# Layer 0 feed forward of a decoder: quarters of a batch against halves, with scaling on POOL and normalisation on ACT

## The chip, the cores and the metric

The kernel runs on one core of one Trainium2 chip. Its time is device microseconds (us) of one execution, and what is told is the median of several runs of the same build. Five engines work side by side and meet only through semaphores: TensorE (PE, its weight loads shown apart as PEld), VectorE (DVE), ScalarE (ACT), GpSimd (POOL) and SyncE (SP, which issues most DMAs). Each engine takes its own instructions strictly in order, so an instruction that waits holds up all that stand behind it on its engine.

## The reference

The input is x of 4 batches x 1024 tokens x 256 channels, with a context of 154 tokens per batch. Two decoder layers follow each other. Each has self attention, cross attention and a feed forward, and after each of the six parts x becomes layernorm(x + part). The change touches the feed forward of layer 0 and the normalisation behind its cross attention. What that feed forward computes:

```
def bit_linear(x, w):                      # act_quant: per token 127 / max|x|, rounded
    xq = x + (act_quant(x) - x)            # weight_quant: one scale, values -1, 0, 1
    wq = w + (weight_quant(w) - w)
    return einsum('bsd,hd->bsh', xq, wq)
h = bit_linear(x, w1)                      # 256 -> 1024
h = depthwise_conv1d(h)                    # three taps along the tokens, plus a bias
h = silu(h)
return bit_linear(h, w2)                   # 1024 -> 256
```

The second `act_quant` needs, for every token, the largest |h| over all 1024 hidden channels before anything can be rounded.

## The kernel before

The kernel has three stages in order of time. The first is layer 0's self attention (to about 690 us from the start of the span). The second is layer 0's cross attention, to about 1328 us, with a long tail. The third is layer 1: a self attention of full width to about 1730 us, then its cross attention and feed forward. The feed forward of layer 0 has no stage of its own. It is woven into the second half of layer 0's cross attention (batches 0 and 1) and into layer 1's self attention (batches 2 and 3).

The weaving is written by hand as events. `at(when, f, args)` puts a small piece of work at a place in a common order, and `run_in_order` calls all pieces in that order. One unit of `when` in the second stage is one call of `scores(s, j)`: four heads of 128 queries against 154 keys. There are 128 of these, 32 to a batch. `schedule(b, t0, length, start)` spreads the feed forward of batch b over `length` units from `t0`, in shares of 100. With `ends = (54, 92, 130, start + 1.2 T, start + 2.8 T)`, `start` 139 and `T` 25, batch 0 has units 54 to 92, batch 1 92 to 130, batch 2 130 to 169, batch 3 169 to 209. PE's instructions and some DMAs keep the order of the program (`tc.keep_in_program_order`). The order on the other engines is laid out by the framework's scheduler when the program is built.

One unit of cross attention: PE forms scores in one of two large PSUM tiles (`slot`); DVE takes their maximum (L810); ACT takes the exponential of four heads with their sums (L814); DVE takes the reciprocal (L818); POOL divides (L822, L825) into one of five `p` tiles; 3.4 units later PE transposes p (L839, L842) into two of four PSUM banks (`bank`), which DVE (L840) and ACT (L843) copy out. Every four units, `weighted` multiplies with the values and ACT copies two `ot` tiles (L860, 15 buffers); every sixteen units, four `out_projected` calls (L862) turn 512 tokens' `ot` into x, at 13.45, 17.45, 21.45 and 23.45 units after their last step, and are followed by `layernorm`.

The feed forward of a batch before the change, in four quarters r of N = 256 tokens:

- `token_scales` (L931, one reduce over the batch), `quantised_x` and `token_rows` (two halves), `edge_tokens`.
- `hidden(b, r, m)`, m from 0 to 3, takes two blocks of 128 hidden channels at once. PE makes 128 x (2 x 256) into one bank, DVE scales it by token into `ht` (L997), ACT fills the two edge columns (L1002) and does the middle tap per block (L1007, 256 columns), DVE the two outer taps per block (L1011, 256 columns each), and ACT a tanh (L1014). `gated` follows on DVE (L1021), with ACT's absolute value (L1026, L1028) and DVE's running maximum (L1029; the two block rows are joined in L1031).
- `hidden_scales` (PE transposes, DVE L1038 and four tiny operations), `quantised_hidden` (PE spreads the scales over all partitions in PSUM, then one DVE multiplication of 128x2048 against that PSUM bank, L1048, and one rounding to bfloat16 of 128x2048, L1051), `fed_forward` (PE, then DVE L1063), `layernorm(b, 2 * r, 2)`.

`layernorm` ends with one instruction per 128 tokens, six events later: on DVE (L169) or, with `scalar=True`, on ACT (L165) after a tiny DVE operation (L160). Before the change only layer 1 passes `scalar=True`. The large tile `gt` of the feed forward has one buffer, as have `xq`, `gq` and `xqT`.

Of the kernel before, what the change touches and what calls it, by code (L numbers as in the profile page):

```python
# [29 lines left out]
def decoder_kernel(ctx: ExitStack, tc: tile.TileContext, a: dict, out: bass.AP):  # L30
# [643 lines left out]
    def wide_cross_attention(wk, wf, slot, bank):  # L674
# [25 lines left out]
        def weight_loaded(name):  # L700
            w = wf.tile([P, 8, E], F32, tag="gt", name="wf", bufs=1).rearrange("p c n -> p (c n)")
            src = a[name].rearrange("(c p) n -> p c n", p=P)
            pe(nc.sync.dma_start(out=w.rearrange("p (c n) -> p c n", c=src.shape[1]), in_=src))
            asum = small.tile([P, 4], F32, tag="asum", name="asum")
            sc = small.tile([P, 1], F32, tag="wsc", name="wsc")
            floats[name] = w, asum, sc
# [138 lines left out]
        def weighted(s):  # L845
# [12 lines left out]
            for i in range(2):  # L858
                ots[s, i] = wk.tile([P, 512], F32, tag="ot", name="ot", bufs=15)
                nc.scalar.copy(ots[s, i], os[i])  # L860

        def out_projected(b, qh, k):  # L862
# [7 lines left out]
            if k == 3:  # L870
                layernorm(b, 4 * qh, 4)
# [19 lines left out]
        for s in range(8 * NB):  # L891
# [6 lines left out]
            if s % 4 == 3:  # L898
                for k in range(4):
                    last = s == 8 * NB - 1  # L900
                    at(4 * s + (10.7 + k if last else (13.45, 17.45, 21.45, 23.45)[k]), out_projected, s // 8, s // 4 % 2, k)


    def feed_forward(wf, bank):
# [7 lines left out]
        scs, dqs, xqTs, rows, edges, gts, ams, sc2s, dq2s, gqs, ths = ({} for _ in range(11))  # L912
        Q = 4
        N = S // Q

        def act_scales(amax, wmean):

            n = amax.shape[1]
            am = small.tile([P, n], F32, tag=f"am{n}", name="am", bufs=2)
            nc.vector.tensor_scalar(am, amax, 1e-5, None, ALU.max)  # L920
            sc = small.tile([P, n], F32, tag=f"sc{n}", name="sc", bufs=2)
            nc.vector.reciprocal(sc, am)
            nc.vector.tensor_scalar(sc, sc, 127.0, None, ALU.mult)
            dq = small.tile([P, n], F32, tag=f"dq{n}", name="dq", bufs=2)
# [3 lines left out]
        def token_scales(b):  # L928
            settle(b)
            amax = small.tile([P, NC], F32, tag="amax", name="amax", bufs=2)  # L930
            nc.vector.tensor_reduce(amax, xs[b], AX.X, ALU.max, apply_absolute_value=True)  # L931
            scs[b], dqs[b] = act_scales(amax, w1m)

        def quantised_x(b, q):
            if q == 0:
                xqTs[b] = wf.tile([P, 2, S], BF16, tag="xqT", name="xqT", bufs=1)
            t = bank(BF16)
            xr = wf.tile([P, 8, N], F32, tag="gt", name="xr", bufs=1)[:, :4, :]
            nc.vector.tensor_tensor(
                xr, xs[b][:, 4 * q : 4 * q + 4, :],  # L940
                scs[b][:, 4 * q : 4 * q + 4].unsqueeze(2).to_broadcast([P, 4, E]), ALU.mult,
            )

            xq = wf.tile([P, 4, E], BF16, tag="xq", name="xq", bufs=1)
            nc.vector.tensor_scalar(xq, xr, RND, RND, ALU.add, ALU.subtract)
            for e in range(2):
                for j in range(4):
                    o = t[:, e * 512 + j * P : e * 512 + (j + 1) * P]
                    pe(nc.tensor.transpose(o, xq[:, j, e * P : (e + 1) * P], ident_bf))
            nc.scalar.copy(xqTs[b][:, :, q * 512 : (q + 1) * 512], t.rearrange("p (e n) -> p e n", e=2))  # L950

        def token_rows(b, q):


            if q == 0:
                rows[b] = wf.tile([P, S], F32, tag="dqr", name="dqr", bufs=1)
            t = bank()
            for j in range(4):
                c = 4 * q + j
                pe(nc.tensor.transpose(  # L960
                    t[:, j * P : (j + 1) * P], dqs[b][:, c : c + 1].to_broadcast([P, P]), ident
                ))
            nc.scalar.copy(rows[b][:, q * 512 : (q + 1) * 512], t)

        def edge_tokens(b):

            t = bank()
            beside = lambda r: r[:, N - 1 : N - 1 + 3 * N].rearrange("p (q n) -> p q n", n=N)[:, :, 0:2]
            for hc in range(8):
                o = t[:, 8 * hc : 8 * hc + 6].rearrange("p (q n) -> p q n", n=2)  # L970
                for e in range(2):
                    mm(o, w1q[:, e, hc * P : (hc + 1) * P], beside(xqTs[b][:, e, :]), e == 0, e == 1)

            ed = edges[b] = wf.tile([P, 8, 2 * Q + 2], F32, tag="ed", name="ed", bufs=1)
            nc.gpsimd.memset(ed, 0.0)
            dq = small.tile([P, 3, 2], F32, tag="dqe", name="dqe", bufs=2)
            nc.vector.tensor_copy(dq, beside(rows[b]))
            nc.vector.tensor_tensor(
                ed[:, :, 2 : 2 * Q],
                t[:, :64].rearrange("p (c n) -> p c n", c=8)[:, :, :6],  # L980
                dq.rearrange("p q n -> p (q n)").unsqueeze(1).to_broadcast([P, 8, 6]), ALU.mult,
            )

        def hidden(b, r, m):
            if m == 0:
                gts[b, r] = wf.tile([P, 8, N], F32, tag="gt", name="gt", bufs=1)
            t = bank()
            for i in range(2):
                hc = 2 * m + i
                for e in range(2):  # L990
                    mm(
                        t[:, i * N : (i + 1) * N], w1q[:, e, hc * P : (hc + 1) * P],
                        xqTs[b][:, e, r * N : (r + 1) * N], e == 0, e == 1,
                    )

            ht = wf.tile([P, 2, N + 2], F32, tag="ht", name="ht", bufs=2)
            nc.vector.tensor_tensor(  # L997
                ht[:, :, 1 : N + 1], t.rearrange("p (i n) -> p i n", i=2),
                rows[b][:, r * N : (r + 1) * N].unsqueeze(1).to_broadcast([P, 2, N]), ALU.mult,
            )  # L1000
            for c, k in ((0, 2 * r), (N + 1, 2 * r + 3)):
                nc.scalar.copy(ht[:, :, c : c + 1], edges[b][:, 2 * m : 2 * m + 2, k : k + 1])  # L1002
            g2 = gts[b, r][:, 2 * m : 2 * m + 2, :]
            for i in range(2):
                hc = 2 * m + i
                g = g2[:, i, :]
                nc.scalar.activation(  # L1007
                    g, ht[:, i, 1 : N + 1], AF.Identity, bias=cb[:, hc : hc + 1], scale=cw[:, hc, 1:2]
                )
                for k in (0, 2):  # L1010
                    nc.vector.scalar_tensor_tensor(  # L1011
                        g, ht[:, i, k : k + N], cw[:, hc, k : k + 1], g, ALU.mult, ALU.add
                    )
            nc.scalar.activation(ht[:, :, :N], g2, AF.Tanh)  # L1014
            ths[b, r, m] = ht

        def gated(b, r, m):

            g2 = gts[b, r][:, 2 * m : 2 * m + 2, :]
            th = ths.pop((b, r, m))  # L1020
            nc.vector.scalar_tensor_tensor(g2, th[:, :, :N], 1.0, g2, ALU.add, ALU.mult)  # L1021
            if m == 0:
                ams[b, r] = wf.tile([P, 2, N], F32, tag="xq", name="am", bufs=1)
            am = ams[b, r]
            if m == 0:
                nc.scalar.activation(am, g2, AF.Abs)  # L1026
            else:
                nc.scalar.activation(th[:, :, :N], g2, AF.Abs)  # L1028
                nc.vector.tensor_tensor(am, am, th[:, :, :N], ALU.max)  # L1029
            if m == 3:  # L1030
                nc.vector.tensor_tensor(am[:, 0, :], am[:, 0, :], am[:, 1, :], ALU.max)  # L1031

        def hidden_scales(b, r):
            t = bank()
            for j in range(2):
                pe(nc.tensor.transpose(t[:, j * P : (j + 1) * P], ams[b, r][:, 0, j * P : (j + 1) * P], ident))
            amax = small.tile([P, 2], F32, tag="amax2", name="amax2", bufs=2)
# [687 lines left out]
```

## Time and profile before

| what | value |
|---|---|
| time, median of 3 runs (lowest to highest) | 2192.05 us (2190.69 to 2195.32) |
| the profiled execution's own time | 2189.57 us |
| its span | 2187.8 us |
| PE, DVE, ACT, POOL busy, share of the span | 94%, 66%, 51%, 27% |
| cross attention with the feed forward of batches 0 and 1 (948 to 1308 us) | PE 329.8, DVE 309.8, ACT 231.6, POOL 170.6 us busy of 360 |
| layer 1 self attention with the feed forward (1327 to 1640 us) | PE 287.8, DVE 243.0, ACT 151.9, POOL 16.7 us busy of 313 |

The busy time of an engine is the union of its instructions. A matmul is pipelined and counts as busy until its modelled end, so PE's share is not a share of its peak. "Idle before, releaser" says how long an engine stood still ahead of a group and what ended that.

### The profile page before, as it was taken

What the parts mean: (1) busy time and instruction counts of PE and PEld (TensorE: products, weight loads), DVE (VectorE), ACT (ScalarE), POOL (GpSimd) and SP (SyncE); (2) the same over time, 40 slices, a digit from 0 to 9 for tenths busy, and PEclk for the clock granted to TensorE, in tenths of its full rate; (3) what the DMA queues carried; (4) which work ended last, traced back from release to release, by engine and by line L of the source; (5) the groups of instructions that cost most, each with busy time, mean ns of one, the idle gap of its engine ahead of it and who ended that gap; (6) DMA issues with size and microseconds to landing.
All of it is one profiled execution on the core that took longest, in us unless ns stands there. A gap on an engine that the chain in (4) does not pass through costs nothing.

```text
span 2187.8 us, 38074 instructions
## 1 busy us (share of the span) xinstructions
PE 2056.9 (94%) x14062; PEld 1221.0 (56%) x14062; DVE 1450.1 (66%) x3179; ACT 1120.3 (51%) x2907; POOL 581.8 (27%) x1211
## 2 busy tenths in 40 slices
PE   7999999999998999989989889899989999999996
PEld 5545545545443556655655556666666655555554
DVE  6666676676673565578987987977762556564634
ACT  1555545545544565566656764545542234544444
POOL 1111231241234655454454442000000310111111
PEclk9999999999999999999999999999999999999998
DMA  4221211211201100000001000000000000010101
GB/s 123 65 56 55 70 36 36 51 36 26 61 27 20 40 21 1 1 1 1 1 1 35 1 23 1 1 1 1 1 1 0 12 15 16 10 30 11 30 1 39
DMA packets 34921, 52.29 MB, mean 24 GB/s; under 512 B 11697, under 2 KB 25905, under 8 KB 34737
## 3 DMA queue, kind: packets, MB, share of 16 engines
q1 hardware_dynamic: 32736, 48.18, 9.0%
q8 instruction: 112, 1.84, 0.3%
q10 hardware_dynamic: 2000, 1.68, 0.3%
q14 instruction: 73, 0.59, 0.1%
HBM read 19.23 MB, written 4.42 MB: 11 GB/s over the span
## 4 chain that ended last, share of the span: by engine, by line
PE 64%; DVE 22%; ACT 6%; POOL 4%; issue 2%; DMA 2%; SPq 1%; ACTq 0%; POOLq 0%; DVEq 0%
PE s L195 18%; PE t L653 14%; PE s L1261 11%; PE s L653 7%; PE acc L195 5%; DVE gt L1011 4%; PE acc L1261 3%; ACT u L814 2%; PE t L839 2%; DVE nmp L361 2%; DVE nmx L810 1%; DVE bnst L136 1%; DVE x L169 1%; DVE ht L997 1%; POOL y L521 1%
## 5 line engine op out<-in xcount | busy, mean ns | idle before, releaser
L422 ACT ACTIVATE p<-s 128x512 f32<-128x512 f32 x576 | 311.8, 596 | 274.6 <-PE s L195 274.1
L361 DVE TENSOR_REDUCE nmp<-s 128x1 f32<-128x512 f32 (+3 forms) x640 | 299.0, 524 | 125.4 <-PE s L195 125.0
L195 PE MATMUL s<-qs,kp 32*128 32x512 f32 (+3 forms) x1536 | 344.3, 521 | 0.8 <-DVE nmp L361 0.8
L195 PE MATMUL s<-kp,qp 32*128 32x128 f32 (+3 forms) x2304 | 325.2, 402 | 2.8 <-DMA qp<-sq 1.5
L822 POOL TENSOR_SCALAR p<-u,rs 128x128 f32<-128x128 f32 x512 | 215.4, 439 | 278.1 <-DVE rs L818 184.8
L195 PEld LDWEIGHTS s<-kp,qp 32*128 32x128 f32 x2304 | 167.2, 184 | 144.2 <-issue 44.2
L814 ACT ACTIVATE u<-s,nmx 128x154 f32<-128x154 f32 x512 | 192.4, 391 | 48.5 <-DVE nmx L810 33.3
L425 POOL TENSOR_SCALAR_AFFINE_SELECT p<-p 128x256 f32<-128x256 f32 x256 | 99.6, 408 | 416.7 <-ACT p L422 386.9
L154 POOL TENSOR_TENSOR rstd<-ve,neghalf 128x4 f32<-128x4 f32 (+1 forms) x56 | 58.1, 1038 | 508.6 <-DVE ve L152 504.0
L195 PE MATMUL acc<-p,v 128*32 128x512 f32 (+3 forms) x1536 | 156.7, 497 | 5.7 <-POOL p L425 4.1
L195 PEld LDWEIGHTS s<-qs,kp 32*128 32x128 f32 x1536 | 139.6, 185 | 32.7 <-DVE nmp L361 15.5
L1418 DVE TENSOR_REDUCE nmt<-s 128x3 f32<-128x462 f32 (+1 forms) x192 | 99.0, 579 | 45.5 <-PE s L1261 45.5
L810 DVE TENSOR_REDUCE nmx<-s 128x4 f32<-128x616 f32 x128 | 100.9, 788 | 39.8 <-PE s L653 38.5
L653 PE MATMUL t<-v,pt 128*128 128x256 f32 x512 | 118.1, 384 | 8.2 <-DVE pt L1170 8.2
L653 PE MATMUL t<-xT,xw 128*128 128x512 f32 x256 | 121.7, 598 | 4.3 <-ACT pr L843 2.0
L1011 DVE SCALAR_TENSOR_TENSOR gt<-ht,cw,gt 128x256 f32<-128x256 f32 x256 | 116.5, 501 | 6.5 <-ACT gt L1007 5.3
L653 PE MATMUL t<-xw,ot 128*128 128x256 f32 x512 | 117.9, 384 | 2.7 <-ACT qt L796 2.6
L653 PEld LDWEIGHTS s<-kt,qt 64*128 64x128 f32 x1024 | 75.9, 186 | 72.7 <-issue 48.9
L653 PE MATMUL s<-qt,xT 128*128 128x512 f32 x256 | 115.2, 592 | 0.0
L653 PEld LDWEIGHTS t<-v,pt 128*128 128x128 f32 x512 | 97.0, 192 | 31.1 <-DVE pt L1170 9.8
L136 DVE BATCH_NORM_STATS2 bnst<-x 128x6 f32<-128x256 f32 x160 | 64.8, 422 | 65.0 <-POOL x L522 43.6
L814 ACT ACTIVATION_READ_ACCUMULATOR u<-s,nmx 128x1 f32 x512 | 106.1, 207 | 0.0
(259 smaller groups left out, 3864.7 us busy)
## 6 DMA issues: line engine op xcount, KB each, us to landing
qs<-qp SPq DMA_DIRECT2D x16, 512.0 KB
qp<-sq SPq DMA_DIRECT2D x124, 64.0 KB
kp<-sk SPq DMA_DIRECT2D x64, 64.0 KB
out_dram<-x SPq DMA_DIRECT2D x8, 512.0 KB
on<-ot SPq DMA_DIRECT2D x60, 64.0 KB
den<-inv SPq DMA_DIRECT2D x56, 64.0 KB
x<-in_x_dram SPq DMA_DIRECT2D x3, 1024.0 KB
wf<-in_L_ffn_w_dram SPq DMA_DIRECT2D x2, 1024.0 KB
```

The costliest lines, as they stand in the source:

```text
L136: nc.vector.bn_stats(st, xs[b][:, c, :])
L195: pe(nc.tensor.matmul(o, l, r, start=start, stop=stop))
L361: nc.vector.tensor_reduce(nmp[:, 2 * pair + g, qc, i : i + 1], t[g][:, c0 : c0 + n], AX.X, ALU.max)
L422: nc.scalar.activation(p[:, g, :], t[g], AF.Exp)
L425: nc.gpsimd.affine_select(out=v, in_=v, compare_op=ALU.is_ge, fill=0.0, base=0, pattern=[[0, 2], [1, P]], channel_multiplier=-1,)
L653: pe(nc.tensor.matmul(o, l, r, start=start, stop=stop))
L810: nc.vector.tensor_reduce(nmx.rearrange("p i g -> p g i"), t, AX.X, ALU.max, negate=True)
L814: nc.scalar.activation(u[:, 2 * i + g, :], t[:, g, i, :], AF.Exp, bias=nmx[:, i, g : g + 1], accum_out=ssum[:, i, g : g + 1],)
L822: nc.gpsimd.tensor_scalar(p[:, h * P : (h + 1) * P], u[:, h, :P], rs[:, h : h + 1], 1.0, ALU.mult, ALU.mult)
L1011: nc.vector.scalar_tensor_tensor(g, ht[:, i, k : k + N], cw[:, hc, k : k + 1], g, ALU.mult, ALU.add)
L1261: pe(nc.tensor.matmul(o, l, r, start=start, stop=stop))
L1418: nc.vector.tensor_reduce(nmts[s % 2][:, 3 * u : 3 * u + n, g, 17], ts[g][:, : n * LK].rearrange("p (c k) -> p c k", k=LK), AX.X, ALU.max, ...
```

## The change

The feed forward works in two halves of N = 512 tokens instead of four quarters of 256, one hidden block of 128 channels at a time, so that the taps and the middle tap have 512 columns and every other operation keeps its 512. The token scales come half by half. The scaling of the hidden values leaves DVE: ACT copies the spread scales from PSUM to an SBUF tile `scr`, and POOL multiplies in four pieces of 128x1024. DVE rounds piece by piece. `fed_forward` is split into four calls of 128 tokens. Both normalisations, the feed forward's and the cross attention's, go to ACT. The tiles `gt` and `gq` grow to 128 x 8 x 512, `ot` has ten buffers instead of fifteen, and `out_projected` moves to 9.45, 11.45, 13.45 and 15.45 units after its last step. The feed forward of batches 0, 1 and 2 starts at units 47, 87 and 127.

```diff
-                ots[s, i] = wk.tile([P, 512], F32, tag="ot", name="ot", bufs=15)
+                ots[s, i] = wk.tile([P, 512], F32, tag="ot", name="ot", bufs=10)
...
-                layernorm(b, 4 * qh, 4)
+                layernorm(b, 4 * qh, 4, True)
...
-                    at(4 * s + (10.7 + k if last else (13.45, 17.45, 21.45, 23.45)[k]), out_projected, s // 8, s // 4 % 2, k)
+                    at(4 * s + (10.7 + k if last else 9.45 + 2 * k), out_projected, s // 8, s // 4 % 2, k)
...
+        def token_scales(b, r):
             settle(b)
+            amax = small.tile([P, M], F32, tag="amax", name="amax", bufs=2)
+            nc.vector.tensor_reduce(
+                amax, xs[b][:, M * r : M * r + M, :], AX.X, ALU.max, apply_absolute_value=True
+            )
+            scs[b, r], dqs[b, r] = act_scales(amax, w1m)
...
+        def hidden(b, r, hc):
+            if hc == 0:
+                gts[b, r] = wf.tile([P, 8, N], F32, tag="gt", name="gt", bufs=1)
+            t = bank()
+            for e in range(2):
+                mm(t, w1q[:, e, hc * P : (hc + 1) * P], xqTs[b][:, e, r * N : (r + 1) * N], e == 0, e == 1)
+
+            ht = hts[b, r, hc] = wf.tile([P, N + 2], F32, tag="ht", name="ht", bufs=2)
+            nc.vector.tensor_tensor(ht[:, 1 : N + 1], t, rows[b, r], ALU.mult)
+            nc.scalar.copy(ht[:, 0 : N + 2 : N + 1], edges[b][:, hc, r : r + 3 : 2])
+            g = gts[b, r][:, hc, :]
+            nc.scalar.activation(g, ht[:, 1 : N + 1], AF.Identity, bias=cb[:, hc : hc + 1], scale=cw[:, hc, 1:2])
+            for k in (0, 2):
+                nc.vector.scalar_tensor_tensor(g, ht[:, k : k + N], cw[:, hc, k : k + 1], g, ALU.mult, ALU.add)
+            nc.scalar.activation(ht[:, :N], g, AF.Tanh)
...
-            g = gts[b, r]
-            nc.vector.tensor_tensor(g, g, t[:, :N].unsqueeze(1).to_broadcast([P, 8, N]), ALU.mult)
-
-            gqs[b, r] = wf.tile([P, 8, N], BF16, tag="gq", name="gq", bufs=1)
-            nc.vector.tensor_scalar(gqs[b, r], g, RND, RND, ALU.add, ALU.subtract)
...
+        def scale_rows(b, r):
+            t = bank()
+            spread_scales(t, sc2s[b, r])
+            scrows[b, r] = wf.tile([P, N], F32, tag="xq", name="scr", bufs=1)
+            nc.scalar.copy(scrows[b, r], t)
+
+        def scaled_hidden(b, r, i):
+            g = gts[b, r][:, 2 * i : 2 * i + 2, :]
+            nc.gpsimd.tensor_tensor(g, g, scrows[b, r].unsqueeze(1).to_broadcast([P, 2, N]), ALU.mult)
+
+        def quantised_hidden(b, r, i):
+            if i == 0:
+                gqs[b, r] = wf.tile([P, 8, N], BF16, tag="gq", name="gq", bufs=1)
+            hc = slice(2 * i, 2 * i + 2)
+            nc.vector.tensor_scalar(gqs[b, r][:, hc, :], gts[b, r][:, hc, :], RND, RND, ALU.add, ALU.subtract)
+
+        def fed_forward(b, r, i):
...
+            measured(b, c)
+            if i == M - 1:
+                layernorm(b, M * r, M, True)
...
+            for r in range(2):
+                u = 10 + 44 * r
+                if r == 1:
+                    on(u - 3, token_rows, 1)
+                for hc in range(8):
+                    on(u + 3.1 * hc, hidden, r, hc)
+                    on(u + 3.1 * hc + 4, gated, r, hc)
+                on(u + 29.5, hidden_scales, r)
+                on(u + 32, scale_rows, r)
+                for i in range(4):
+                    on(u + 33 + 1.7 * i, scaled_hidden, r, i)
+                    on(u + 35.5 + 1.7 * i, quantised_hidden, r, i)
+                    on(u + 42.5 + 1.2 * i, fed_forward, r, i)
...
-        ends = (54.0, 92.0, 130.0, start + 1.2 * T, start + 2.8 * T)
+        ends = (47.0, 87.0, 127.0, start + 1.2 * T, start + 2.8 * T)
```

## The prediction, made before the changed kernel ran

> **What bounds the kernel now.** I read the page's busy shares first, then busy time by stretch, the costliest groups of the stretch where cross attention and the feed forward overlap, PE's waits there, the chain, and two short timelines. The stretches (columns: length, then PE, PEld, DVE, ACT, POOL busy, granted clock):
>
> ```profile
> 735.00:925.00 190.00, 188.81 (x1115) 115.59 (x1113) 110.51 (x234) 112.03 (x489) 103.73 (x268) 1.00 0.02 7
> 948.00:1308.00 360.00, 329.84 (x1979) 210.25 (x1979) 309.75 (x655) 231.58 (x871) 170.63 (x369) 0.98 0.03 9
> 1327.00:1640.00 313.00, 287.77 (x1382) 203.23 (x1381) 242.99 (x540) 151.94 (x308) 16.74 (x17) 0.99 0.00 1
> 1640.00:1730.00 90.00, 89.31 (x369) 62.36 (x368) 29.96 (x63) 26.61 (x43) 4.45 (x7) 1.00 0.01 1
> ```
>
> Without the feed forward (first and last row) PE has no hole and DVE is busy 58% and 33%. With it (middle rows) PE stands 30 us of 360 and 25 us of 313, and DVE is at 86% and 78%. The groups of 948 to 1308 us (count, then busy and mean ns):
>
> ```profile
> L1011 DVE SCALAR_TENSOR_TENSOR gt<-ht,cw,gt 128x256 f32<-128x256 f32 x128 | 61.6, 523 | 4.4 <-ACT gt L1007 3.8
> L1021 DVE SCALAR_TENSOR_TENSOR gt<-ht,gt 128x512 f32<-128x512 f32 x31 | 21.7, 701 | 2.2 <-ACT ht L1014 1.8
> L1048 DVE TENSOR_TENSOR gt<-gt,t 128x2048 f32<-128x2048 f32 x7 | 15.9, 2278 | 0.2 <-PE t L1044 0.2
> L743 POOL TENSOR_TENSOR x<-x,bo 128x256 f32<-128x256 f32 x16 | 11.9, 772 | 7.4 <-PE t L737 7.3
> L825 POOL TENSOR_TENSOR p<-u,rs 128x104 f32<-128x104 f32 x68 | 27.9, 410 | 0.0
> ```
>
> The taps are DVE's dearest group: 256 columns cost 0.52 us, 512 only 0.70. PE's waits there (total, times, longest) go to DVE, or to ACT behind DVE:
>
> ```profile
> PE t L653 <- ACT qt L796: 7.3, 5, 2.1
> PE t L653 <- DVE pt L840: 4.3, 5, 1.4
> PE t L1044 <- DVE sc L923: 4.1, 2, 3.3
> PE t L653 <- DVE ht L997: 3.7, 4, 1.3
> ```
>
> The chain changes sides within each quarter (start, length, what): PE alone, then 30 us where DVE and ACT carry it.
>
> ```profile
> 1077.24 3.46 PE t L653 x16
> 1080.70 0.72 PE s L653 x8
> 1082.12 3.92 PE t L653 x24
> ...
> 1095.60 0.71 DVE nmx L810
> 1097.51 0.60 DVE ht L997
> 1098.22 0.64 DVE qt L794
> 1098.86 2.04 DVE gt L1011 x4
> 1100.90 1.29 DVE x L169 x4
> ```
>
> So DVE time there is worth something, but the hidden blocks come in bursts, and only what thins the burst counts.
>
> **The change part by part.** The sum stands against the profiled execution, 2189.6 us, which is 2.5 below the median of 2192.05.
>
> *DVE, per batch.* Taps: 64 x 0.50 (page mean 501 ns) become 32 x 0.69 (L1021's 701 and 676 ns): 32.1 to 22.1, -10.0. Scaling, 4 x 2.28 (L1048): -9.1. Rounding, 4 x 1.22 (L1051) to 8 x 0.70 (L945, the same 128x1024, 711 and 682 ns): +0.7. Running maximum, 12 x 0.70 and 4 x 0.45 to 14 x 0.70: -0.4. Scales of the hidden values, four sets of about 1.13 (L1038 0.41, four tiny ones 0.72) to two of 1.4: -1.8. Normalisation, 8 x 0.43 (L169) to two tiny ones, with two `ve` fewer: -3.4. Token scales in two: +0.8. Together -23.2; the cross attention's normalisation gives -3.1 more. Four batches: -105 us of DVE's 1450.
>
> *ACT, per batch.* Middle tap 32 x 0.60 (L1007) to 16 x 0.84 (0.60 plus 256 columns at 0.94 ns, the slope from L1014's 512 in 0.63 to L1158's 1024 in 1.11): -5.7. Edges -3.2, `scr` +1.2, sixteen normalisations at 0.59 (L165): +9.5. Net +2 on an engine with 36% idle. But four normalisations come in a row, 2.4 us in front of the exponentials, sixteen times. Bounds 0 (covered by the 3.4 units between scores and transposes) and 1.2 each; I take 0.3: **+5**.
>
> *The cross attention stretch.* L810's reduces give the pace: 48th at 903.2, 128th at 1315.7, 412.5 us for 80 units. Per half of 20 units afterwards: hidden blocks spread over 25.7% of 40 units, 10.3 units. DVE needs 8 x 3.5 = 28.0 (0.68 + 1.40 + 0.70 + 0.73) plus 10.3 x 1.95 of its own (L810 0.79, L840 0.68, L818 0.17, queries and keys 0.31): 48.1, at 98% packing (durations in 948 to 1308 add up to 352 of 360) 49.3. About 11 of the 20 `out_projected` calls of these units now fall into these stretches, 1.03 us of DVE each. Four halves: 208. The other 38.8 units hang on PE: 3.05 each (units 8 to 20 ran at 2.96), feed forward 4 x 5.5 (32 matmuls of 0.11 make 3.5, spreads and transposes 2), nine `out_projected` at 16 x 0.216: 171, with 5% of waits 180. Sum 388: **-24**. Bounds: 0, if the hidden burst is held by its own chain of five hand-overs as now, and -45, if the work levels out at PE's 4.6 a unit.
>
> *Layer 1's self attention.* DVE falls from 243 to 197 of 313 us. Of PE's 25 us of holes I take half: **-13** (0 to -25).
>
> *The scaling on POOL*, the change's price. A piece of 128x1024: L825 has 104 elements in 0.36 us and L743 256 in 0.73 when DVE leaves them alone, 2.4 ns per element, so 2.6 us. Bounds: 1.1 (half of DVE's own 2.28) and 2.9 (four L743). In the built instruction order seven of eight halves carry all four pieces in a row on POOL, 10.4 us, where the kernel before had 3.5 on DVE. Queued behind them on POOL are the next unit's divisions, for which PE's transposes wait; DVE's roundings wait for them, and behind these on DVE stand the next unit's maximum, PSUM copy and reciprocal. With scores of a unit ended at 0, its division ends at 4.9 (0.8 maximum, 4 x 0.365 exponentials, 0.17, 2.1), pieces end at 7.5, 10.1, 12.7, 15.3. DVE does two roundings, then the maximum due at 4.4 starts at 10.8, PT's copy at 11.6, the last rounding ends near 16, and only then the next reciprocal. PE has four banks and two slots, about one unit of 4.4, to run ahead: it stands about 5 us. In layer 1's stage POOL is free, but four roundings stand in one block with the next maximum behind them, about 12 us with 2.8 us of work in it, against 7.8 us of PE work per 128 queries: again about 5. With half a microsecond for a granted clock that drops after a hole (0.86 in the slice 925 to 950 us, where PE waits longest), 5.5 x 8: **+44**. Bounds 1 each, where PE has work in hand, and 10 each, the whole block.
>
> The trace has a further cost, not in the sum: POOL and DVE shut each other out. Three divisions (0.37 each alone) took 2.20 beside a rounding, and a gate of 0.68 took 0.91 behind a POOL addition:
>
> ```profile
> 1195.56 2.20 POOL L822 TENSOR_SCALAR p<-u,rs 128x128 f32<-128x128 f32 x3 [2.82 <-DVE rs L818]
> 1195.62 1.20 DVE L1051 TENSOR_SCALAR gq<-gt 128x2048 bf16<-128x2048 f32 x1
> ...
> 965.27 2.55 POOL L743 TENSOR_TENSOR x<-x,bo 128x256 f32<-128x256 f32 x3
> 965.64 0.91 DVE L1021 SCALAR_TENSOR_TENSOR gt<-ht,gt 128x512 f32<-128x512 f32 x1
> ```
>
> The Trainium skill ("SBUF — State Buffer", section "Who interferes with whom") makes this a rule: VectorE in a two-port mode or with two SBUF inputs and GpSimd reading SBUF hold one pair of ports exclusively, and the later one waits for the whole instruction. That speaks against this change, for each rounding would then meet the next piece; by the rule the blocks would run one behind the other, 10.4 + 2.8 instead of 10.4 + 0.7, some 2 us more eight times, +16. "GPSIMD Engine Reference", section "Performance versus the Vector engine", has 4497 ns for 2048 elements on GpSimd, so an estimate of 2.3 us a piece; by that the POOL term would be about 5 us smaller. I take neither.
>
> *The rest.* PE's columns stay the same (64 x 256 against 32 x 512). The feed forward's first transposes wait for half a reduce less: **-2** (0 to -4). Ten `ot` buffers: the sixth step's copy, at unit 27.9, reuses what `out_projected` freed on PE at 27.45, in PE's own order, so nothing; if that fails, one matmul group of 3.5 us in a few places. SP's queue issues the same DMAs.
>
> Sum: -24 - 13 + 44 + 5 - 2 = +10, so 2199.6, and 2202 at the median's level. I say 2201.
>
> **The rivals.**
> *The relief comes through.* PE covers the POOL blocks with work in hand, at about 1 us each (+8 instead of +44): -26, 2166 at the median's level, to 2185 when they cost 3.4 each. For it: PE's longest waits for the scaling's steps are 3.3 us now (L1044 for L923) and 3.7 in layer 1's stage (for L1051), and most quarters pass with less. Against: the maximum stands behind the roundings on DVE. It decides from 4.2 us a block downwards, where the sum is zero. Chance 0.33.
> *The ports.* Each POOL piece also shuts out DVE, and blocks cost 8 to 10: +20 to +36 more, 2221 to 2237. For it the timeline above; against it that POOL has been the one to wait in most of such meetings. Chance 0.15.
> *Nothing to measure*, gains and blocks cancel: 2188 to 2196. Chance 0.10.
> *My case*, blocks of 4.9 to 7.9 us, 2197 to 2220: 0.42.
>
> **How the numbers follow.** A measurement of this kernel can tell about 0.2% (4.4 us) from no change. Slower takes my case and the ports, 0.57; faster 0.33; same 0.10. The range reaches over all four, from 2168 to 2236, with a tenth left out on each side; my case's own range is 2197 to 2220.
>
> **What would show it.** DVE busy should fall by about 100 us; 128x512 taps should take 0.69; a POOL piece 2.3 to 2.9; PE should name POOL's division or DVE's maximum and copies as its releasers right after each row of four pieces, with holes near 5 us; the pace between them should be under 5 us a unit. I am wrong if those holes stay under 4 us, if the hidden stretches keep their pace of over 5 us because the hand-overs and not DVE's time hold them, or if ACT becomes the engine that PE waits for.

## The result and the profile after

The changed kernel takes 2226.01 us against 2191.47 us for the kernel before, run beside it: a ratio of 1.0154 with a 95% interval of 1.0136 to 1.0171. It is slower by 34.5 us where 9.5 were forecast. The profiled execution has a span of 2226.5 us (2187.8 before).

In the new file the two outer taps are L1001 (L1011 before), the gate L1008 (L1021), the running maximum L1014 (L1029), the transposes of the hidden scales L1019 (L1036), the scaling L1032 (L1048), the rounding L1038 (L1051), layer 1's maximum L1142 (L1156) and its transposes L1155 (L1169).

Busy time by stretch, cut at the same work as before (columns: length, then PE, PEld, DVE, ACT, POOL busy, granted clock, DMA share, GB/s):

```profile
735.00:925.00 190.00, 188.21 (x1140) 117.22 (x1138) 114.21 (x245) 117.14 (x495) 101.67 (x263) 1.00 0.02 7
925.00:1345.00 420.00, 370.64 (x2094) 234.18 (x2107) 320.02 (x604) 258.53 (x930) 225.51 (x425) 0.95 0.03 8
1345.00:1680.00 335.00, 296.03 (x1302) 201.63 (x1312) 234.39 (x430) 157.07 (x278) 54.43 (x33) 0.94 0.00 1
1680.00:1770.00 90.00, 89.30 (x370) 62.45 (x369) 30.57 (x64) 26.85 (x43) 4.45 (x7) 1.00 0.00 1
```

Before, the second of these stretches was:

```profile
925.00:1327.00 402.00, 363.67 (x2188) 232.14 (x2185) 342.79 (x717) 253.07 (x956) 189.45 (x410) 0.97 0.03 9
```

The stretches without the feed forward are as they were. Cross attention with the feed forward took 402 us and takes 420. Layer 1's self attention beside the feed forward took 313 us and takes 335; PE stood 25 us in it and stands 39, and its granted clock fell from 0.99 to 0.94. By the starts of the maxima, the 125th unit of cross attention begins at 1334.1 instead of 1308.3 (+25.8), and the last of layer 1's self attention at 1764.5 instead of 1723.6 (+41). So both stages lose, and what follows gives a little back.

The groups of DVE and POOL that the change made, 925 to 1685 us (count, then busy and mean ns, then the engine's idle time before them and what ended it):

```profile
L1001 DVE SCALAR_TENSOR_TENSOR gt<-ht,cw,gt 128x512 f32<-128x512 f32 x128 | 96.9, 759 | 10.4 <-ACT gt L999 9.6
L1032 POOL TENSOR_TENSOR gt<-gt,scr 128x1024 f32<-128x1024 f32 x32 | 79.6, 2516 | 74.5 <-ACT scr L1028 74.5
L1038 DVE TENSOR_SCALAR gq<-gt 128x1024 bf16<-128x1024 f32 x32 | 65.6, 2085 | 31.2 <-POOL gt L1032 31.2
L1008 DVE SCALAR_TENSOR_TENSOR gt<-ht,gt 128x512 f32<-128x512 f32 x64 | 44.6, 697 | 5.0 <-ACT ht L1002 4.3
```

A POOL piece is 2.52 us (2.6 forecast). The rounding, which the same 128x1024 form does in 0.70 us elsewhere (L945 before), shows 2.09 us, and DVE stood another 31.2 us in front of it waiting for POOL: the 32 roundings hold DVE for 96.8 us instead of 22. PE's waits, 925 to 1345 us (total, times, longest):

```profile
PE t L653 <- DVE pt L840: 11.4, 9, 3.3
PE t L842 <- DVE pt L840: 10.9, 4, 7.0
```

The copy of the transposed probabilities (L840), 5.5 us of PE's waits before (4.3 at L653 and 1.2 at L842), is now over 22. How it comes about is seen in the chain from 988 to 1012 us (start, length, what), around the first row of POOL pieces in batch 0:

```profile
991.56 2.31 POOL gt L1032
...
993.89 8.02 DVE gq L1038 x2
1001.91 0.72 DVE nmx L810
...
1004.38 4.82 PE s L653 x24
```

and in the timeline of the same place (start, length, instructions; in brackets idle time before and releaser):

```profile
991.51 9.25 POOL L1032 TENSOR_TENSOR gt<-gt,scr 128x1024 f32<-128x1024 f32 x4
993.89 8.02 DVE L1038 TENSOR_SCALAR gq<-gt 128x1024 bf16<-128x1024 f32 x2 [4.84 <-POOL gt L1032]
1001.83 0.79 DVE L810 TENSOR_REDUCE nmx<-s 128x4 f32<-128x616 f32 x1
...
1003.37 0.45 PE L842 MATMUL t<-ident,p 128*128 128x128 f32 x1 [7.05 <-DVE pt L840]
```

DVE's next maximum (L810) and copy (L840) stand behind two roundings, the roundings behind POOL; PE has used up its work and stands 7.05 us. That is the hole the prediction described (5 us), where it described it. The eight rows are uneven: in the 16 us from the start of a row PE stands 7.6, 3.9, 7.5 and 5.6 us in cross attention and 1.9, 1.4, 3.2 and 6.7 in layer 1. In three of the rows two roundings stand ahead of the next maximum, in five all four.

### The profile page after: what moved, and what is told of

Its sections match the earlier page's. It is cut to its first block, busy times and chain, and to the rows that moved or that the text cites. A ratio compares the mean times of both kernels' runs of the same rounds, so it can differ in the third digit from the quotient of the medians.

```text
span 2226.5 us, 37569 instructions
## 1 busy us (share of the span) xinstructions
PE 2070.8 (93%) x13912; PEld 1223.7 (55%) x13942; DVE 1423.6 (64%) x2967; ACT 1135.2 (51%) x2851; POOL 652.7 (29%) x1235
## 4 chain that ended last, share of the span: by engine, by line
PE 66%; DVE 17%; ACT 7%; POOL 5%; issue 2%; DMA 1%; SPq 0%; ACTq 0%; POOLq 0%; DVEq 0%
PE s L195 18%; PE t L653 16%; PE s L1247 10%; PE s L653 8%; PE acc L195 5%; PE acc L1247 3%; DVE gq L1038 3%; DVE gt L1001 2%; ACT u L814 2%; PE t L839 2%; ACT x L165 2%; DVE nmp L361 2%; DVE bnst L136 1%; POOL gt L1032 1%; PE t L1155 1%
## 5 line engine op out<-in xcount | busy, mean ns | idle before, releaser
L822 POOL TENSOR_SCALAR p<-u,rs 128x128 f32<-128x128 f32 x512 | 212.7, 433 | 270.6 <-DVE rs L818 157.0
L154 POOL TENSOR_TENSOR rstd<-ve,neghalf 128x4 f32<-128x4 f32 x48 | 50.6, 1054 | 379.4 <-DVE ve L152 375.0
L653 PE MATMUL t<-xT,xw 128*128 128x512 f32 x256 | 124.5, 610 | 6.9 <-ACT ot L860 2.3
L810 DVE TENSOR_REDUCE nmx<-s 128x4 f32<-128x616 f32 x128 | 101.0, 789 | 46.1 <-PE s L653 45.4
L653 PE MATMUL t<-xw,ot 128*128 128x256 f32 x512 | 120.3, 390 | 6.9 <-DVE pt L840 3.3
L653 PE MATMUL s<-qt,xT 128*128 128x512 f32 x256 | 120.9, 617 | 0.2 <-issue 0.2
L136 DVE BATCH_NORM_STATS2 bnst<-x 128x6 f32<-128x256 f32 x192 | 78.4, 422 | 65.0 <-POOL x L522 43.1
L653 PE MATMUL t<-v,pt 128*128 128x256 f32 x512 | 116.3, 381 | 3.1 <-DVE pt L1156 3.0
L653 PEld LDWEIGHTS s<-kt,qt 64*128 64x128 f32 x1024 | 78.0, 190 | 73.6 <-issue 53.9
L653 PEld LDWEIGHTS t<-v,pt 128*128 128x128 f32 x512 | 96.6, 190 | 26.1 <-issue 6.9
L653 PEld LDWEIGHTS t<-xw,ot 128*128 128x128 f32 x512 | 98.4, 196 | 22.7 <-DVE pt L840 3.7
```

Of the source, the lines that this page charges most:

```text
L136: nc.vector.bn_stats(st, xs[b][:, c, :])
L653: pe(nc.tensor.matmul(o, l, r, start=start, stop=stop))
L810: nc.vector.tensor_reduce(nmx.rearrange("p i g -> p g i"), t, AX.X, ALU.max, negate=True)
L822: nc.gpsimd.tensor_scalar(p[:, h * P : (h + 1) * P], u[:, h, :P], rs[:, h : h + 1], 1.0, ALU.mult, ALU.mult)
```

## The experiments

**Who does the scaling.** The first theory: the four pieces on POOL are the loss, and the rest of the change gains. The rival: the rest does not gain either.

```diff
-            nc.gpsimd.tensor_tensor(g, g, scrows[b, r].unsqueeze(1).to_broadcast([P, 2, N]), ALU.mult)
+            nc.vector.tensor_tensor(g, g, scrows[b, r].unsqueeze(1).to_broadcast([P, 2, N]), ALU.mult)
```

> The changed kernel with one edit: the four pieces of scaling run on DVE instead of POOL (same tiles, same places). Pieces theory (the row of pieces on POOL and DVE's roundings, which they shut out, cause most of the 34.5 us): 2190 to 2203, and the roundings of 128x1024 go from 1.9 us mean back to 0.7. Bursts theory (the halves bunch DVE's work whatever does the scaling): 2215 to 2235, since DVE gets 8 x 1.23 us per batch more.

Measured: 2173.01 us, ratio 0.9913 (0.9896 to 0.9929) to before. With the scaling on DVE the change is 18.0 us faster than before, so the scaling on POOL costs 52.5 us against the scaling on DVE. The kernel is faster than either theory expected. The groups of this kernel, 925 to 1660 us:

```profile
L1032 DVE TENSOR_TENSOR gt<-gt,scr 128x1024 f32<-128x1024 f32 x32 | 39.2, 1243 | 2.9 <-ACT scr L1028 2.9
L1038 DVE TENSOR_SCALAR gq<-gt 128x1024 bf16<-128x1024 f32 x32 | 22.0, 701 | 0.0
```

Scaling and rounding together hold DVE for 64.1 us, less than the rounding alone held it in the changed kernel. That the pieces are the loss holds; the gain of the rest is smaller than the 34 us of the forecast's other terms.

**Port, order, or POOL's queue.** Three mechanisms could make these 52.5 us: the roundings meeting POOL's pieces at a port, DVE standing in its own order behind POOL, or POOL's divisions coming late. The first kernel rounds once, 128x4096, behind all four pieces, so that no rounding runs beside a piece:

```diff
-            if i == 0:
-                gqs[b, r] = wf.tile([P, 8, N], BF16, tag="gq", name="gq", bufs=1)
-            hc = slice(2 * i, 2 * i + 2)
+            if i < 3:
+                return
+            gqs[b, r] = wf.tile([P, 8, N], BF16, tag="gq", name="gq", bufs=1)
+            hc = slice(0, 8)
```

> The changed kernel, scaling on POOL, but one rounding of 128x4096 behind all four pieces instead of four roundings between them. Port theory (a rounding that meets the next piece waits for the whole of it, and the next piece for the rounding: 9.4 us of pieces become 12 and more): 8 to 15 us faster than 2226, 2211 to 2218, and pieces of 2.35 us throughout. Queue theory (what counts is that DVE stands until the pieces are done, and POOL's divisions behind them): within 6 us of 2226.

Measured: 2224.61 us, ratio 1.0152 (1.0136 to 1.0167): the time of the changed kernel. Its groups, 925 to 1650 us:

```profile
L1032 POOL TENSOR_TENSOR gt<-gt,scr 128x1024 f32<-128x1024 f32 x32 | 74.3, 2355 | 76.8 <-ACT scr L1028 76.8
...
L1039 DVE TENSOR_SCALAR gq<-gt 128x4096 bf16<-128x4096 f32 x8 | 18.4, 2294 | 67.1 <-POOL gt L1032 67.1
```

The pieces and the rounding run undisturbed, and DVE stands 67.1 us for POOL instead: rounding and wait hold it for 85.5 us, against 96.8. The meeting at the port is gone and the time is not. This does not clear the port in the changed kernel's own rows, since one rounding behind all four pieces waits as long for its data. In the row shown above the second piece had ended at 996.16; without the port the two roundings ahead of the maximum could have been through by 996.9 (an estimate: that end and 0.7 us of rounding) instead of 1001.91. In the five rows where all four roundings stand together, the last of them ends within 0.9 us of the last piece's end and 0.7 us, so there the port costs little.

The second kernel keeps the pieces on POOL and where they are, and takes DVE's wait away: the roundings are placed later, and they and the two maxima keep the order of the program (`pe(...)`, as PE's instructions do):

```diff
-                    on(u + 35.5 + 1.7 * i, quantised_hidden, r, i)
-                    on(u + 42.5 + 1.2 * i, fed_forward, r, i)
+                    on(u + 40 + 0.5 * i, quantised_hidden, r, i)
+                    on(u + 44.5 + 1.2 * i, fed_forward, r, i)
...
-            nc.vector.tensor_reduce(nmx, s, AX.X, ALU.max, negate=True)
+            pe(nc.vector.tensor_reduce(nmx, s, AX.X, ALU.max, negate=True))
```

(the same `pe(...)` stands around L810 and L1038.)

> The changed kernel, scaling on POOL, with the four roundings 4.5 to 3.3 shares (about 1.5 units, 7 us) later, the output projection of the feed forward 2 shares later, and the roundings and the maxima L810 and L1142 pinned to the order of the program on DVE, so that DVE goes on with the next units' maxima while POOL scales. If DVE's standing is the cost: 20 to 45 us faster, 2181 to 2206. If POOL's late divisions are the cost: within 10 us of 2226.

Measured: 2179.17 us, ratio 0.9948 (0.9933 to 0.9963). Its groups, 925 to 1632 us:

```profile
L1032 POOL TENSOR_TENSOR gt<-gt,scr 128x1024 f32<-128x1024 f32 x32 | 74.4, 2356 | 72.3 <-ACT scr L1028 72.3
...
L1038 DVE TENSOR_SCALAR gq<-gt 128x1024 bf16<-128x1024 f32 x32 | 22.1, 734 | 0.0
```

POOL does the same 74 us in the same rows, its divisions are queued behind them as before, and DVE waits 0.0 for them. Against the kernel before this is -12.5 us where the changed kernel has +34.5: 47.0 us for DVE's wait. In the 16 us from the start of each row PE now stands 3.0 us in all, where the changed kernel has 37.7. The divisions stay late, and this loss is gone all the same; PE names POOL for none of its waits from 925 to 1690 us. What POOL's row still costs here stays open: DVE is busy for 29 us less than with the scaling on DVE (1385.7 against 1414.5), and the kernel is 6 us slower.

The third kernel moves nothing and only has the `pe(...)`:

```diff
-            nc.vector.tensor_scalar(gqs[b, r][:, hc, :], gts[b, r][:, hc, :], RND, RND, ALU.add, ALU.subtract)
+            pe(nc.vector.tensor_scalar(gqs[b, r][:, hc, :], gts[b, r][:, hc, :], RND, RND, ALU.add, ALU.subtract))
```

> The changed kernel with nothing moved in the written order; only the roundings and the maxima L810 and L1142 are pinned to that order on DVE. In the changed kernel as built two roundings stand ahead of the maximum that follows the scaling; here two more maxima come first. If the built order is most of the cost: 2180 to 2195. If the written places, too close behind POOL's pieces, are: 2205 to 2226.

Measured: 2183.87 us, ratio 0.9977 (0.9968 to 0.9986). The same place in its timeline:

```profile
991.07 9.27 POOL L1032 TENSOR_TENSOR gt<-gt,scr 128x1024 f32<-128x1024 f32 x4
995.34 0.80 DVE L810 TENSOR_REDUCE nmx<-s 128x4 f32<-128x616 f32 x1
996.65 4.92 DVE L1038 TENSOR_SCALAR gq<-gt 128x1024 bf16<-128x1024 f32 x2
```

The maximum now runs at 995.3, in the middle of POOL's row, instead of at 1001.8 behind it. The first of the two roundings behind it still takes 4.3 us beside POOL's pieces. So the order of DVE's roundings and maxima is worth 39 of the 47 us, and the events' places the rest. The program's events had the maximum ahead of the roundings; the framework's scheduler, which lays out every engine but PE, put two roundings in front of it.

**What the port costs by itself.** With the scaling on DVE, POOL is given eight products per half that nobody reads, two behind each call of the scaling:

```diff
+            for _ in range(2):
+                nc.gpsimd.tensor_tensor(dum, scrows[b, r], scrows[b, r], ALU.mult)
```

(`dum` is 128x512 in bfloat16; 64 products in all.)

> The changed kernel with the scaling on DVE (2173.0), and on POOL in the same places, for nothing, eight products of 128x512 per half (about 10 us) that no one waits for; the computation itself is unchanged. It measures what the block on POOL costs by itself, by the divisions behind it and by the ports, without DVE's wait for the scaled values. If POOL's late divisions are most of the 53 us: 2205 to 2230. If DVE's standing is: 2173 to 2190.

Measured: 2202.70 us, ratio 1.0055 (1.0034 to 1.0076), 29 us more than the same kernel without them, and between the two ranges expected. Its groups, 925 to 1690 us:

```profile
L1035 POOL TENSOR_TENSOR dum<-scr 128x512 bf16<-128x512 f32 x64 | 98.1, 1533 | 79.8 <-ACT scr L1029 75.6
...
L1033 DVE TENSOR_TENSOR gt<-gt,scr 128x1024 f32<-128x1024 f32 x32 | 52.9, 1670 | 2.9 <-ACT scr L1029 2.9
...
L1041 DVE TENSOR_SCALAR gq<-gt 128x1024 bf16<-128x1024 f32 x32 | 37.0, 1168 | 0.0
```

DVE's product grew from 1243 to 1670 ns and its rounding from 701 to 1168 ns with no wait for data: 28.6 us over the 64 instructions. POOL's work takes DVE's time where DVE has work of its own. How much of the 29 us is this and how much the divisions queued behind the idle products (PE waited 5.8 us for L822 here) is not told apart.

**Normalisation on ACT**, taken back from the changed kernel, and done alone on the kernel before:

```diff
-                layernorm(b, 4 * qh, 4, True)
+                layernorm(b, 4 * qh, 4)
...
-                layernorm(b, M * r, M, True)
+                layernorm(b, M * r, M)
```

> The changed kernel with both normalisations back on DVE, nothing else. Pieces theory: the normalisations on ACT matter little, within 6 us of 2226. Theory of the ACT bursts (four normalisations in a row in front of the exponentials): at least 10 us faster, below 2216.

Measured: 2219.36 us, ratio 1.0125 (1.0110 to 1.0140).

> The kernel before with only the normalisations moved to ACT (in twos for the feed forward's quarters, in fours behind the cross attention). Pieces theory and my term for this part: 3 to 8 us faster (27 us of DVE gone, 0.3 us lost per burst on ACT), 2184 to 2189. Theory of the ACT bursts: 10 us slower or more.

Measured: 2193.90 us, ratio 1.0013 (1.0004 to 1.0022). The move to ACT costs 6 us in the changed kernel and 3 on the kernel before. Both together with the scaling on DVE:

> The changed kernel with scaling and both normalisations on DVE: what is left of the change are the halves, the 512 column taps and the ten buffers. If the two single edits add up (53.0 and 6.7 us): 2164 to 2170. If DVE becomes the bound again by the 27 + 10 us per batch that it gets back: above 2180.

Measured: 2169.61 us, ratio 0.9902 (0.9886 to 0.9919), 4 us better than the scaling alone. And with late roundings, where DVE has the most room:

> Scaling on POOL with the later, pinned roundings (2179.2), and both normalisations on DVE. If the normalisations cost on ACT what the two pairs before showed (6.7 and 3.4 us): 2172 to 2176, so POOL would still be no better a place for the scaling than DVE (2169.6), though DVE has 40 us less to do. If DVE's time is what bounds: below 2169.

Measured: 2180.57 us, ratio 0.9964 (0.9951 to 0.9977), against 0.9948 with ACT: about 4 us the other way. The intervals of this pair overlap, and so do those of the pair with the scaling on DVE. Of the four runs only 2169.61 lies in a range that was expected. So what ACT's turn is worth hangs on the arrangement and has no fixed sign; all four are small.

**Ten buffers and the earlier `out_projected`**, alone on the kernel before:

```diff
-                ots[s, i] = wk.tile([P, 512], F32, tag="ot", name="ot", bufs=15)
+                ots[s, i] = wk.tile([P, 512], F32, tag="ot", name="ot", bufs=10)
...
-                    at(4 * s + (10.7 + k if last else (13.45, 17.45, 21.45, 23.45)[k]), out_projected, s // 8, s // 4 % 2, k)
+                    at(4 * s + (10.7 + k if last else 9.45 + 2 * k), out_projected, s // 8, s // 4 % 2, k)
```

> The kernel before with only ten buffers of the output tiles and the output projection at 9.45, 11.45, 13.45 and 15.45 units. My term was nothing for the buffers. Theory that the projections now bunch PE's and DVE's work onto the hidden stretches: 5 to 15 us slower. Pieces theory: within 5 us of 2191.5.

Measured: 2196.07 us, ratio 1.0022 (1.0012 to 1.0032): +5 us, at the edge of both ranges expected. The 25th maximum is at 808.5 us (803.3 before), but the first units lose nothing: two projections now stand ahead of it that stood behind. At the 53rd and the 69th maximum, where both kernels have made equally many projections (8 and 12), this one is 0.7 and 1.7 us ahead. At the 128th it is 5.0 us behind, with 28 projections made instead of 26. The tail from there to layer 1's first maximum has two fewer and takes 68.2 us instead of 67.3, so the 5 us are not given back. Buffers and places were not tried one by one.

**What DVE's time is worth.** The prediction held the stretches with hidden blocks for DVE's. So a whole outer tap was left out, with the scaling and normalisation on DVE, and then on the kernel before:

```diff
-            for k in (0, 2):
+            for k in (0,):
```

> The changed kernel with scaling and normalisations on DVE (2169.6), and without the second outer tap: 64 operations of 128x512, 48 us of DVE, all of them in the stretches of hidden blocks. This leaves out the third tap of the convolution, so its time is that of a smaller computation. Step of my prediction (those stretches are bound by DVE's time at 98%): 35 to 48 us faster. If their chain of hand-overs or PE bounds them: 0 to 20 us faster.

Measured: 2141.62 us, ratio 0.9788 (0.9772 to 0.9804). 48 us of DVE instructions are gone and 25 us of time (-47.4 against -22.1 us, each to its own kernel before), between the two ranges expected. DVE's busy time, in which neighbours that overlap count once, fell by 43 us (1432.9 to 1389.7).

> The kernel before without the second outer tap: 128 operations of 128x256, 64 us of DVE. This leaves out the third tap of the convolution. If the kernel before is bound by DVE's time wherever the feed forward runs: 45 to 64 us faster than 2191.5. If only its bursts count: 10 to 35 us.

Measured: 2157.91 us, ratio 0.9861 (0.9846 to 0.9876): 31 us for 64 us of DVE instructions, or for 48 us of busy time (1450.1 to 1402.0). A microsecond of DVE's busy time is worth about 0.6 us, not a whole one, in both arrangements (0.58 and 0.65). The tap that is gone was also a link of the chain between ACT and DVE, which these runs do not tell apart.

**Where layer 1's stage loses.** PE's waits from 1320 us on show one cause the prediction did not name. The changed kernel:

```profile
PE t L1019 <- DVE am L1014: 11.0, 2, 5.9
PE t L1155 <- ACT p L1144: 9.4, 4, 6.7
```

The kernel with scaling and normalisation on DVE, in which no row of POOL pieces is left:

```profile
PE t L1019 <- DVE am L1014: 14.2, 3, 5.2
```

The transposes of the running maximum (L1019) stand in PE's fixed order, and the last of eight hidden blocks ends late on DVE. Before the change the same line (L1036 for L1031) had 1.3 us. The kernels with late roundings and with only the order pinned show the same 11.0 us at L1019 as the changed kernel, while the 9.4 us at L1155, behind the row of roundings, are 0.2 and 0.7 there. So the stand at L1019 comes with every variant of the change, whatever does the scaling, and L1155 belongs to POOL's row. If L1019 eats the gain, PE should be given other work first: in batches 2 and 3 the scales and what follows them are put three shares later.

```diff
-                on(u + 29.5, hidden_scales, r)
-                on(u + 32, scale_rows, r)
+                d = 0 if t0 + length < start else 3
+                on(u + 29.5 + d, hidden_scales, r)
+                on(u + 32 + d, scale_rows, r)
...
-                    on(u + 33 + 1.7 * i, scaled_hidden, r, i)
-                    on(u + 35.5 + 1.7 * i, quantised_hidden, r, i)
-                    on(u + 42.5 + 1.2 * i, fed_forward, r, i)
+                    on(u + 33 + d + 1.7 * i, scaled_hidden, r, i)
+                    on(u + 35.5 + d * 2 / 3 + 1.7 * i, quantised_hidden, r, i)
+                    on(u + 42.5 + d / 2 + 1.2 * i, fed_forward, r, i)
```

> The changed kernel with scaling and normalisations on DVE (2169.6), and for batches 2 and 3 the transposes of the running maximum, the spread of the scales and the scaling 3 shares (1.2 units, about 4 us) later, the roundings 2 and the last projection 1.5 shares later. If PE's stand at those transposes (L1019, three waits of 14.2 us together and clock that drops behind them) is what ate the relief in layer 1's self attention: 6 to 15 us faster, 2155 to 2164. If the wait only moves to the next thing behind the same burst of hidden blocks: within 4 us of 2169.6.

Measured: 2157.32 us, ratio 0.9858 (0.9844 to 0.9873): 10 us better than without (0.9902), and the fastest complete kernel here, 1.4% under the kernel before. PE's waits from 1310 to 1632 us, and the stretch of layer 1's self attention:

```profile
PE t L1019 <- DVE am L1014: 5.0, 1, 5.0
```

```profile
1310.00:1620.00 310.00, 295.75 (x1357) 203.30 (x1353) 237.57 (x472) 150.56 (x265) 15.21 (x20) 0.98 0.00 1
```

Two of the three holes are gone. The edit moves the scaling and the roundings too, so the 10 us are not the transposes' alone. The granted clock follows: by the trace's clock records, from the last maximum of cross attention to the last of layer 1's self attention, PE ran at half speed for 6.8 us before the change, 37.5 us in the changed kernel, 23.9 us with scaling and normalisation on DVE, and 10.2 us here. The same step with the scaling on POOL, roundings late and the normalisation on ACT:

```diff
-                    on(u + 35.5 + 1.7 * i, quantised_hidden, r, i)
-                    on(u + 42.5 + 1.2 * i, fed_forward, r, i)
+                    on(u + 40 + d * 2 / 3 + 0.5 * i, quantised_hidden, r, i)
+                    on(u + 44.5 + d / 3 + 1.2 * i, fed_forward, r, i)
```

> Scaling on POOL with later, pinned roundings (2179.2), and for batches 2 and 3 the transposes of the maximum and the scaling 3 shares later, as with the scaling on DVE, where that was worth 12.3 us. If the stand at L1019 ate the relief there too: 2163 to 2173. If that gain belonged to the other arrangement: 2175 to 2183.

Measured: 2166.95 us, ratio 0.9904 (0.9887 to 0.9920), 9 us better than 0.9948 without it; half speed 10.2 us in the same stretch, where late roundings alone have 30.7. With every wait mended that was found, the scaling on POOL is still behind the scaling on DVE (0.9904 against 0.9858), though it takes some 40 us of products off DVE. The two kernels differ in the normalisation too, so these 10 us are not one part's price. The earlier start of the feed forward (units 47, 87 and 127) and the halves were not tried alone.

## Why the prediction was right or wrong, step by step

The direction was right, the size not: 2226.0 against 2201, and outside my case's own 2197 to 2220, though inside the range. The time lies in the interval of the rival with the ports, 2221 to 2237, but that rival needed blocks of 8 to 10 us. They cost 5.9 each (47.0 over eight), as in my case (4.9 to 7.9); what failed is the relief that was to stand against them.

*The scaling on POOL, +44: right in sum.* The row of pieces with DVE's roundings, maximum and copy behind it costs 47.0 us (changed kernel against late roundings, so without what POOL's row may still cost there). The holes are 4.7 us a row in the mean and between 1.4 and 7.6, four of them under the 4 us that were named as a sign of being wrong. The terms up to the division's end add up to 4.5 us, where the step says 4.9. What the step had wrong is where it put the cause: it took the order "two roundings, then the maximum" for a given of four pieces in a row, and it is a choice of the scheduler. With the program's own order most of the cost is gone, with the pieces still on POOL. Late divisions, the other half of the step's argument, are not most of these 47 us, since they stay in the kernel with late roundings; what they cost by themselves was not measured.

*The ports, not in the sum: their share stays open.* They do shut out DVE: the first rounding of batch 0 took 7.42 us instead of 0.68, which put the maximum behind it back by some 5 us. The rounding behind all four pieces gives the same total, but it holds DVE as long, so it does not tell the port from the order; with the program's order the roundings still meet the pieces and most of the loss is gone. Where DVE has work of its own, the port costs a part of the 29 us of the idle products. The Trainium skill ("SBUF — State Buffer", section "Who interferes with whom") has the exclusive pair; the longer DVE instructions beside the idle products (1670 ns for 1243, 1168 for 701) agree with it.

*The cross attention stretch, -24: this failed, by size.* From the 48th to the 128th maximum, the forecast's own stretch, the kernel before took 412.5 us and the one with late roundings 399.7: -13. The working said DVE bounds the hidden stretches "at 98% packing". That figure added durations (352 us), while the row of stretches shown in the same prediction has DVE busy for 309.75 of 360 us: neighbouring DVE records overlap, by 0.08 us at the taps (L794 starts at 1098.14 and lasts 0.72, the next record starts at 1098.78). In the kernel with scaling and normalisation on DVE the four hidden stretches together take 198 us for 38 units, 5.2 a unit where the forecast had 5.05 (208 over 41.2). So the pace of over 5 us stayed, which was named as a sign of being wrong. PE is 93% and DVE 90% busy in them: at that density DVE no longer decides alone, which is what one tap, worth 0.6 of its busy time, shows from the other side. The rest was forecast at 180 us for 38.8 units, 4.6 a unit, and takes 201 for 42 (399.0 less 198), 4.8 a unit.

*Its tap price, 0.69 us: wrong.* The outer taps, which take a per-partition weight, last 0.759 at 512 columns; 0.697 is what the gate takes, a different operand, and it was the gate that I read. And 0.50 us for 256 columns overlapped with its neighbour: between 700 and 1770 us the taps were busy for 116.5 us before and 97.7 with late roundings, -19 and not -40. The scales' -7 did come: the five operations of the hidden scales add up to 18.4 us in 16 sets before and to 11.3 in 8 sets with late roundings. DVE's whole busy time falls by 64 us (1450.1 to 1385.7 with late roundings), not 105; in the changed kernel by 26, as the profile counts a rounding that stands at the port as busy.

*Layer 1's self attention, -13: this failed, by size.* With late roundings, where POOL's rows leave PE no hole in this stage, it gains 1 us (from the first maximum to the last, 340.6 us before and 339.5). The step took PE's holes for DVE's load and did not ask which instruction PE would stand at when eight hidden blocks end together: L1019, 11 us, and a clock at half speed around it. With the scales and what follows three shares later the stage takes 332.2 us: -8. The changed kernel's 359.8 us hold the same 11 us and, on top, the POOL term's share.

*ACT's bursts, +5: not measured by itself.* The move to ACT costs between -4 and +6 us by arrangement, but this is the net with DVE's relief, which had been counted as a gain elsewhere.
*Ten buffers, 0: wrong by 5 us.* The argument on the sixth step's copy looked at one buffer's reuse and not at where the projections go: two of them move from the tail, which got no shorter without them, to ahead of the last unit. That is read from the maxima and not shown by an experiment of its own.

*The sum.* Without the POOL term the forecast had -34; late roundings show -12.5, the buffers' 5 us included. That difference of some 21 us, with 3 us more at POOL, is the miss of 25. It lies in the two reliefs, forecast at -37 together and measured at -14.

## What to carry to other kernels

When work moves to a slower engine, look in the built order at what the waiting engine has next behind its wait, and pin that order before judging the move: here roundings ahead of a maximum cost 39 us and turned a small gain into a loss. An engine's load is the union of its instructions in the stretch, never the sum of their durations; and where another engine is over 90% busy beside it, do not count a microsecond saved as a whole one: here it was worth about 0.6. When a burst gets larger, ask which in-order instruction waits for its last member, and move that one later by as much.

## What the runs showed of the hardware

- In the changed kernel one DVE rounding of 128x1024, whose data were there at 993.87 us, lasted 7.42 us for 0.68 us of work, until POOL's three further pieces had ended (1000.76 us): it was not let in between them. The three behind it took 0.68 us each. In six of the other seven rows the first rounding took 2.82 to 2.84 us, so it came in behind one piece. Over all 32 the mean is 2.09 us.
- POOL multiplies 128x1024 in float32 in 2.36 us when DVE is quiet (with late roundings, or with one rounding), 2.52 when roundings meet it; DVE needs 1.24 us for the same.
- Short holes at PE cost clock as well: the hole of 7.05 us that ended at 1003.37 us has a half clock record from 1001.1 to 1007.9. In layer 1's stage time at half clock went from 6.8 to 37.5 us with three holes of 5 to 7 us, and was 10.2 in the two kernels with the scales put later, which have one such hole.
